# A depthwise convolution on sixteen 32x32 tiles of TensorE, four channels at once

## The chip, the cores and the metric

The kernel runs on one core of one Trainium2 chip. The metric is the device time of one launch in microseconds (us): the median of three runs of the kernel before is 9306.91 us (9300.4 to 9478.17). Views of the profile come from one more execution, recorded with the hardware profiler.

## The reference

A layer of ConvNeXt style with a mixture of experts, then an attention within each token, then a second mixture, on an image batch of 32 x 128 x 56 x 56 in float32. The change lies in the first step alone, a depthwise 7x7 convolution (each channel has its own 49 weights):

```python
x = jax.lax.conv_general_dilated(input, dw_kernel, (1, 1), ((3, 3), (3, 3)),
        feature_group_count=C, dimension_numbers=('NCHW', 'OIHW', 'NCHW')) + dw_bias[None, :, None, None]
x = jnp.transpose(x, (0, 2, 3, 1))
mu = x.mean(-1, keepdims=True)          # layer norm over the 128 channels, and so on
...
```

Everything after it (norm, choice of experts, both mixtures, attention) reads the convolution's result and is the same in both kernels.

## The kernel before

**The convolution as matrix products.** The rows of an image lie on the partitions of SBUF, 56 of them for one channel, and along a partition lie the 32 images with 62 columns each (56 and 3 of padding on both sides). Summing over the 7 rows of the filter is a product with a banded 56x56 matrix, one for each column of the filter (`band`, read backwards into `br`). The 7 columns of the filter are 7 shifted readings of the same tile, accumulated in PSUM. Even and odd output columns are computed with a trick that saves products: `products(c, 0)` takes the 4 even taps of the filter on every second column of the input ("evens"), `products(c, 1)` the 3 odd ones ("odds", 29 columns instead of 28 for each image), and `products(c, 2)` works on `xs`, the sums of neighbouring columns, with the sums of neighbouring bands ("boths", 4 taps). The even outputs are evens + odds, and the odd ones boths - evens - odds, with odds shifted by one.

**Tiles.** Two channels are worked on at once: channel `c` on partitions 0 to 55, channel `c + 64` on partitions 64 to 119. TensorE's array is cut into eight tiles of 64 rows x 32 columns. Row group `r` belongs to one channel. The four column groups `q` belong to the even and odd output rows (`i`) and to the two halves of the image batch (`b`). Each product has one PSUM tile of a bank for each channel (`cps`); the pool has eight banks.

**One turn of the loop over `c`** (64 turns): SyncE's queue starts two loads of bands (L256) and two of x (L262, `xin <- in_x_dram`, packets of one image row, 224 bytes); VectorE turns the bands round (L265, `br <- band`), GpSimd adds bands (L269) and makes `xs` (L273); TensorE works through evens, odds and boths (L244). ScalarE copies evens out of PSUM to `ea` (L281). VectorE makes the even outputs from odds in PSUM and `ea` (L285, twice per channel), replaces `ea` by boths + bias - `ea` (L289), and takes odds off again for the odd outputs (L294, twice). ScalarE's queue then starts the output's way to DRAM (L299, `conv_d <- ot`, two output rows in a packet of 448 bytes). Loads land in three rotating buffers (`nbuf`).

**Order.** Instructions on one engine run in the order that the compiler's scheduler gave them when the kernel was built, which need not be that of the text; a DMA that is started from ScalarE's queue stands in the same queue as ScalarE's copies. The next stage reads all 128 channels of a token from `conv_d` (`ct <- conv_d`, L446) and starts when the convolution has ended.

Of the kernel before, what the change touches and what calls it, by code (L numbers as in the profile page):

```python
# [8 lines left out]
F32 = mybir.dt.float32  # L9
# [3 lines left out]
ALU = mybir.AluOpType  # L13
# [4 lines left out]
P = 128  # L18
GJ = 7
GT = P * GJ  # L20
KS = 7
PAD = 3
# [3 lines left out]
def conv_attn_hybrid_kernel(  # L26
# [173 lines left out]
    HH, QP = H // 2, P // 4  # L200
    assert H <= HP and N % 2 == 0 and W % 2 == 0 and NB * (WH + 1) * 4 <= 2048
    assert H % 2 == 0 and HH <= QP
    with tc.tile_pool(name="cv_c", bufs=1) as cc, tc.tile_pool(
# [13 lines left out]
        bands = [cc.tile([P, KS, 2 * H], F32, name=f"band{i}") for i in range(nbuf)]  # L217
        turned_bands = [cc.tile([P, KS + NO, 2, QP], F32, name=f"br{i}") for i in range(nbuf)]
        xins = [cc.tile([P, N, WP], F32, name=f"xin{i}") for i in range(nbuf)]
        for i in range(nbuf):  # L220
            nc.vector.memset(bands[i], 0.0)
            nc.vector.memset(turned_bands[i], 0.0)
            nc.gpsimd.memset(xins[i], 0.0)
        cview = conv_d.rearrange("n c (h w) -> c h n w", w=2 * W)

        def products(c, part):

            bt, xi, xs = turned_bands[c % nbuf], xins[c % nbuf], sums_of_x[c]
            wide = WH + (part == 1)
            pss = [cvp.tile([P, NB, wide], F32, name="cps") for r in range(2)]  # L230
            taps = NO if part == 1 else NE
            for a in range(taps):
                for r in range(2):
                    rows = slice(r * HP, r * HP + H)
                    for b in range(2):
                        imgs = slice(b * NB, (b + 1) * NB)
                        if part < 2:
                            at_ = 2 * a + part
                            w_, m_ = at_, xi[rows, imgs, at_ : at_ + 2 * wide - 1 : 2]
                        else:  # L240
                            w_, m_ = (0, KS, KS + 1, KS + 2)[a], xs[rows, imgs, a : a + WH]
                        for i in range(2):
                            q = i * HP + b * QP
                            nc.tensor.matmul(  # L244
                                pss[r][q : q + QP], bt[rows, w_, i, :], m_,
                                start=(a == 0), stop=(a == taps - 1),
                                tile_position=(r * HP, q), skip_group_check=True,
                            )
# [3 lines left out]
        for c in range(CH):  # L252
            bt, br, xi = bands[c % nbuf], turned_bands[c % nbuf], xins[c % nbuf]
            for r in range(2):
                rows, cr = slice(r * HP, r * HP + H), r * CH + c
# [1624 lines left out]
```

## Time and profile before

| | |
|---|---|
| median of three runs | 9306.91 us |
| profiled execution: time | 9293.81 us |
| profiled execution: span, first to last instruction | 9292.1 us |
| TensorE matmul busy, whole span | 8361.1 us (90%) |
| VectorE / ScalarE / GpSimd busy, whole span | 71% / 57% / 75% |
| mean granted TensorE clock | 0.93 |
| output DMAs of the convolution (`conv_d <- ot`) issued | from 26.3 to 606.5 us |

How to read it: a row of a table of windows gives, for a stretch of time in us from the span's start, the busy time of each engine with the number of its instructions, the granted clock, the mean busy share of the 16 DMA engines (over 1 means that packets overlap) and GB/s. PE is TensorE's matmul, PEld its weight load, DVE VectorE, ACT ScalarE, POOL GpSimd, SP SyncE; a q behind the name is the engine's queue, where DMAs are issued. A float32 matmul appears as two records. A row of the groups by line gives line, engine, operation, out<-in by the program's names, shapes, count, then busy us and mean ns of one, then the idle time before and who ended it. Rows of the timeline begin with start and duration in us; neighbours of a kind are merged, with their number behind an x.

### The profile page before, as it was taken

How to read it: one execution, taken by the hardware profiler on the slowest of the kernel's cores; microseconds unless marked ns; L12 is line 12 of the kernel's file. 1: busy time of each engine (PE TensorE's matmuls, PEld its weight loads, DVE VectorE, ACT ScalarE, POOL GpSimd, SP SyncE). 2: the span in 40 equal slices, each digit the busy share in tenths (PEclk: the TensorE clock that was granted, in tenths of full speed). 3: DMA queues.
4: the chain of work that ended last, by engine and by line, in shares of the span. 5: the costliest groups of instructions: out<-in, count | busy, mean ns of one | idle time of the engine just before them, and what ended most of it. 6: DMA issues, size and time to landing. Idle time of an engine off the chain costs nothing. (4 is left out here: it accounts for less than half of the span.)

```text
span 9292.1 us, 168854 instructions
## 1 busy us (share of the span) xinstructions
PE 8361.1 (90%) x64890; PEld 6953.7 (75%) x64890; DVE 6606.0 (71%) x9020; ACT 5293.3 (57%) x13300; POOL 7015.2 (75%) x4994
## 2 busy tenths in 40 slices
PE   9996667666999999996999999999999999999879
PEld 5676455554777777775899999999999999999733
DVE  7779766665222222225999999999999999999623
ACT  1138322332333333334888888888888888888600
POOL 2235466665888888888999999999999999999500
PEclk9998788888999999998999999999999999999855
DMA  9984255555544444442000000000000000000299
GB/s 205 217 212 152 84 159 173 167 174 144 77 73 72 69 72 67 72 71 32 25 30 32 32 32 28 29 32 28 32 32 32 25 32 32 28 32 32 74 319 339
DMA packets 867126, 829.22 MB, mean 89 GB/s; under 512 B 403157, under 2 KB 758808, under 8 KB 846835
## 3 DMA queue, kind: packets, MB, share of 16 engines
q1 hardware_dynamic: 459410, 473.36, 18.2%
q0 software_dynamic: 177664, 188.81, 11.9%
q10 hardware_dynamic: 229248, 156.26, 5.7%
q8 instruction: 514, 8.42, 0.4%
q14 instruction: 290, 2.37, 0.1%
HBM read 465.46 MB, written 353.64 MB: 88 GB/s over the span
## 5 line engine op out<-in xcount | busy, mean ns | idle before, releaser
L161 POOL TENSOR_TENSOR s<-s,q 128x2048 f32<-128x2048 f32 x784 | 3600.2, 4609 | 54.1 <-DVE s L161 32.1
L161 DVE TENSOR_TENSOR s<-kv,c 128x2048 f32<-128x2048 f32 x784 | 1793.6, 2288 | 20.8 <-POOL c L161 19.2
L161 POOL DMA_INDIRECT t_d<-ys,xe x992 | 1543.2, 1556 | 331.4 <-issue 275.8
L161 DVE TENSOR_TENSOR ev<-s,kv 128x2048 f32<-128x2048 f32 x784 | 1789.8, 2283 | 1.0 <-ACT s L161 1.0
L161 ACT ACTIVATE s<-s 128x2048 f32<-128x2048 f32 x784 | 1505.9, 1921 | 463.4 <-POOL s L161 459.3
L161 PE MATMUL sm<-ident,s 128*128 128x128 f32 x12544 | 1525.2, 275 | 71.6 <-DVE oT L161 64.0
L161 PE MATMUL sm<-ident,ev 128*128 128x128 f32 x12544 | 1520.1, 275 | 1.4 <-DVE ev L161 1.4
L161 PEld LDWEIGHTS sm<-ident,s 128*128 128x128 f32 x12544 | 1398.6, 143 | 93.9 <-issue 73.7
L161 PEld LDWEIGHTS sm<-ident,ev 128*128 128x128 f32 x12544 | 1429.7, 143 | 45.9 <-DVE ev L161 3.0
L1132 ACT ACTIVATE hT<-ph,b1t 128x512 f32<-128x512 f32 (+1 forms) x992 | 679.8, 685 | 1129.6 <-PE ph L161 1122.4
L1149 DVE TENSOR_TENSOR ys<-py,b2t 128x512 f32<-128x512 f32 (+1 forms) x248 | 171.5, 692 | 1399.4 <-PE py L161 1295.5
L863 POOL DMA_INDIRECT xb_d<-xs,rd x784 | 766.0, 977 | 497.9 <-DVE xs L161 233.5
L161 PEld LDWEIGHTS py<-w,hT 128*128 128x128 f32 x7936 | 924.1, 191 | 116.9 <-issue 63.7
L161 PE MATMUL py<-w,hT 128*128 128x128 f32 x7936 | 925.3, 275 | 0.0
L161 PE MATMUL ph<-xeT,w 128*128 128x512 f32 (+1 forms) x1984 | 904.4, 599 | 0.0
L161 PEld LDWEIGHTS ph<-xeT,w 128*128 128x128 f32 x1984 | 364.1, 194 | 362.6 <-issue 359.1
L161 ACT COPY add<-px 128x512 f32<-128x512 f32 x224 | 116.0, 533 | 854.2 <-remote 474.7
L161 DVE SCALAR_TENSOR_TENSOR xs<-pa,rst,add 128x256 f32<-128x256 f32 x784 | 328.8, 479 | 344.1 <-issue 126.9
L161 PE MATMUL pa<-rw,ct 128*128 128x256 f32 x1568 | 405.1, 407 | 175.9 <-DVE xs L161 146.7
L161 PEld LDWEIGHTS pa<-rw,ct 128*128 128x128 f32 x1568 | 317.8, 207 | 295.2 <-remote 133.3
L161 PE MATMUL kv<-wq,zT 128*128 128x256 f32 x1568 | 418.6, 390 | 53.1 <-DVE ev L161 53.1
L244 PE MATMUL cps<-xin,br 56*32 56x448 f32 (+1 forms) x7168 | 440.9, 585 | 18.2 <-POOL xs L273 13.4
(348 smaller groups left out, 13723.4 us busy)
## 6 DMA issues: line engine op xcount, KB each, us to landing
ct<-conv_d SPq DMA_DIRECT2D x192, 448.0 KB
xin<-in_x_dram SPq DMA_DIRECT2D x128, 392.0 KB
conv_d<-ot ACTq DMA_DIRECT2D x256, 196.0 KB
t_d<-xs ACTq DMA_DIRECT2D x112, 448.0 KB
tr<-t_d SPq DMA_DIRECT2D x112, 448.0 KB
to<-t_d SPq DMA_DIRECT2D x32, 1568.0 KB
out_dram<-oo ACTq DMA_DIRECT2D x32, 1568.0 KB
xg<-in_x_dram SPq DMA_DIRECT2D x96, 448.0 KB
```

What stands on the lines that cost most here:

```text
L161: r = getattr(self.engine, name)(*a, **k)
L244: nc.tensor.matmul(pss[r][q : q + QP], bt[rows, w_, i, :], m_, start=(a == 0), stop=(a == taps - 1), tile_position=(r * HP, q), skip_group ...
L863: s = nc.gpsimd.indirect_dma_start(out=xb_d, out_offset=bass.IndirectOffsetOnAxis(ap=idx, axis=0), in_=row, in_offset=None, bounds_check=R ...
L1132: nc.scalar.activation(hT[:, f, :, :rows], ph[:, :, :rows], AF.Gelu, bias=b1t[:, f : f + 1])
L1149: nc.vector.tensor_tensor(ys[:rows], py[:rows], across(b2t, SB)[:rows], ALU.add)
```

## The change

Four channels are worked on at once (`R4`), in 32 turns instead of 64. A partition now holds two neighbouring rows of an image (`pi`), so a channel needs 28 of 32 partitions, and the array is cut into sixteen tiles of 32 rows x 32 columns. Each tap needs two matmuls, one for each of the two rows on a partition. A product has four PSUM tiles, one for each channel, in the same pool of eight banks.

The two rows lie next to each other in DRAM, so x is loaded in packets of 448 bytes into a tile `raw` without padding (three buffers); ScalarE copies `raw` into the padded `xin` (two buffers). Bands are loaded with every second row and the row after it for each partition. `xs` has two buffers instead of three. VectorE turns and GpSimd adds bands for each of the two rows apart.

ScalarE now copies odds to SBUF as well (`od`), and both copies stand in the text right behind their product; VectorE's two operations on odds read `od` instead of PSUM. The sums, their order for one output, and the way out to DRAM are as before.

```diff
--- before.py
+++ after.py
@@ -197,7 +197,7 @@
     WH, CH = W // 2, C // 2
     NE, NO = (KS + 1) // 2, KS // 2
     BL = (KS - 1) * 2 * H + H
-    HH, QP = H // 2, P // 4
+    HH, QP, R4 = H // 2, P // 4, 4
     assert H <= HP and N % 2 == 0 and W % 2 == 0 and NB * (WH + 1) * 4 <= 2048
     assert H % 2 == 0 and HH <= QP
     with tc.tile_pool(name="cv_c", bufs=1) as cc, tc.tile_pool(
@@ -214,76 +214,96 @@
         nc.sync.dma_start(bias, dw_bias.partition_broadcast(P))
 
         nbuf = 3
-        bands = [cc.tile([P, KS, 2 * H], F32, name=f"band{i}") for i in range(nbuf)]
-        turned_bands = [cc.tile([P, KS + NO, 2, QP], F32, name=f"br{i}") for i in range(nbuf)]
-        xins = [cc.tile([P, N, WP], F32, name=f"xin{i}") for i in range(nbuf)]
+        bands = [cc.tile([P, 2, KS * 2 * H], F32, name=f"band{i}") for i in range(nbuf)]
+        turned_bands = [cc.tile([P, 2, KS + NO, 2, QP], F32, name=f"br{i}") for i in range(nbuf)]
+        raws = [cc.tile([P, N, 2, W], F32, name=f"raw{i}") for i in range(nbuf)]
+        xins = [cc.tile([P, N, 2, WP], F32, name=f"xin{i}") for i in range(2)]
         for i in range(nbuf):
             nc.vector.memset(bands[i], 0.0)
             nc.vector.memset(turned_bands[i], 0.0)
-            nc.gpsimd.memset(xins[i], 0.0)
+            nc.gpsimd.memset(raws[i], 0.0)
+        for xi in xins:
+            nc.gpsimd.memset(xi, 0.0)
         cview = conv_d.rearrange("n c (h w) -> c h n w", w=2 * W)
 
         def products(c, part):
 
-            bt, xi, xs = turned_bands[c % nbuf], xins[c % nbuf], sums_of_x[c]
+            bt, xi, xs = turned_bands[c % nbuf], xins[c % 2], sums_of_x[c]
             wide = WH + (part == 1)
-            pss = [cvp.tile([P, NB, wide], F32, name="cps") for r in range(2)]
+            pss = [cvp.tile([P, NB, wide], F32, name="cps") for r in range(R4)]
             taps = NO if part == 1 else NE
             for a in range(taps):
-                for r in range(2):
-                    rows = slice(r * HP, r * HP + H)
-                    for b in range(2):
-                        imgs = slice(b * NB, (b + 1) * NB)
-                        if part < 2:
-                            at_ = 2 * a + part
-                            w_, m_ = at_, xi[rows, imgs, at_ : at_ + 2 * wide - 1 : 2]
-                        else:
-                            w_, m_ = (0, KS, KS + 1, KS + 2)[a], xs[rows, imgs, a : a + WH]
-                        for i in range(2):
-                            q = i * HP + b * QP
-                            nc.tensor.matmul(
-                                pss[r][q : q + QP], bt[rows, w_, i, :], m_,
-                                start=(a == 0), stop=(a == taps - 1),
-                                tile_position=(r * HP, q), skip_group_check=True,
-                            )
+                for pi in range(2):
+                    for r in range(R4):
+                        rows = slice(r * QP, r * QP + HH)
+                        for b in range(2):
+                            imgs = slice(b * NB, (b + 1) * NB)
+                            if part < 2:
+                                at_ = 2 * a + part
+                                w_, m_ = at_, xi[rows, imgs, pi, at_ : at_ + 2 * wide - 1 : 2]
+                            else:
+                                w_, m_ = (0, KS, KS + 1, KS + 2)[a], xs[rows, imgs, pi, a : a + WH]
+                            for i in range(2):
+                                q = i * HP + b * QP
+                                nc.tensor.matmul(
+                                    pss[r][q : q + QP], bt[rows, pi, w_, i, :], m_,
+                                    start=(a == 0 and pi == 0), stop=(a == taps - 1 and pi == 1),
+                                    tile_position=(r * QP, q), skip_group_check=True,
+                                )
             return pss
 
         sums_of_x = {}
-        for c in range(CH):
-            bt, br, xi = bands[c % nbuf], turned_bands[c % nbuf], xins[c % nbuf]
-            for r in range(2):
-                rows, cr = slice(r * HP, r * HP + H), r * CH + c
+        for c in range(C // R4):
+            bt, br, raw, xi = bands[c % nbuf], turned_bands[c % nbuf], raws[c % nbuf], xins[c % 2]
+            for r in range(R4):
+                rows, cr = slice(r * QP, r * QP + HH), r * (C // R4) + c
                 nc.sync.dma_start(
-                    bt[rows].rearrange("p a b -> p (a b)")[:, :BL],
+                    bt[rows, :, :BL],
                     bass.AP(
-                        band_d.tensor, band_d.offset + cr * KS * 2 * H, [[1, H], [1, BL]]
+                        band_d.tensor, band_d.offset + cr * KS * 2 * H,
+                        [[2, HH], [1, 2], [1, BL]],
                     ),
                 )
                 nc.sync.dma_start(
-                    xi[rows, :, PAD : PAD + W], x[:, cr].rearrange("n h w -> h n w")
-                )
-            nc.vector.tensor_copy(
-                br[:, :KS, :, :HH],
-                bt[:, :, :H][:, :, ::-1].rearrange("p k (h i) -> p k i h", i=2),
-            )
-            nc.gpsimd.tensor_tensor(
-                br[:, KS:, :, :HH], br[:, 2:KS:2, :, :HH], br[:, 1 : KS - 1 : 2, :, :HH], ALU.add
-            )
-            xs = sums_of_x[c] = cv.tile([P, N, WP // 2], F32, name="xs")
-            nc.gpsimd.tensor_tensor(xs, xi[:, :, 0::2], xi[:, :, 1::2], ALU.add)
+                    raw[rows].rearrange("p n i w -> p n (i w)"),
+                    x[:, cr].rearrange("n (h i) w -> h n (i w)", i=2),
+                )
+            for pi in range(2):
+                nc.vector.tensor_copy(
+                    br[:, pi, :KS, :, :HH],
+                    bt[:, pi].rearrange("p (a b) -> p a b", a=KS)[:, :, :H][:, :, ::-1].rearrange(
+                        "p k (h i) -> p k i h", i=2
+                    ),
+                )
+                nc.gpsimd.tensor_tensor(
+                    br[:, pi, KS:, :, :HH], br[:, pi, 2:KS:2, :, :HH],
+                    br[:, pi, 1 : KS - 1 : 2, :, :HH], ALU.add,
+                )
+            nc.scalar.copy(xi[:, :, :, PAD : PAD + W], raw)
+            xs = sums_of_x[c] = cv.tile([P, N, 2, WP // 2], F32, name="xs", bufs=2)
+            nc.gpsimd.tensor_tensor(xs, xi[:, :, :, 0::2], xi[:, :, :, 1::2], ALU.add)
             evens = products(c, 0)
+            eas = []
+            for r in range(R4):
+                ea = cv.tile([P, NB, WH], F32, name="ea", bufs=2 * R4)
+                nc.scalar.copy(ea, evens[r])
+                eas.append(ea)
             odds = products(c, 1)
+            ods = []
+            for r in range(R4):
+                od = cv.tile([P, NB, WH + 1], F32, name="od", bufs=2 * R4)
+                nc.scalar.copy(od, odds[r])
+                ods.append(od)
             boths = products(c, 2)
-            ot = cv.tile([P, NB, 2, W], F32, name="ot", bufs=3)
-            for r in range(2):
-                cr = r * CH + c
-                ea = cv.tile([P, NB, WH], F32, name="ea", bufs=4)
-                nc.scalar.copy(ea, evens[r])
-                mine = slice(r * HP, (r + 1) * HP)
+            for r in range(R4):
+                cr, ea, od = r * (C // R4) + c, eas[r], ods[r]
+                if r % 2 == 0:
+                    ot = cv.tile([P, NB, 2, W], F32, name="ot", bufs=3)
+                mine = slice(r % 2 * HP, (r % 2 + 1) * HP)
                 for i in range(2):
                     of = slice(i * HP, (i + 1) * HP)
                     nc.vector.scalar_tensor_tensor(
-                        ot[mine, :, i, 0::2], odds[r][of, :, :WH], bias[of, cr : cr + 1], ea[of],
+                        ot[mine, :, i, 0::2], od[of, :, :WH], bias[of, cr : cr + 1], ea[of],
                         ALU.add, ALU.add,
                     )
                 nc.vector.scalar_tensor_tensor(
@@ -292,10 +312,10 @@
                 for i in range(2):
                     of = slice(i * HP, (i + 1) * HP)
                     nc.vector.tensor_tensor(
-                        ot[mine, :, i, 1::2], ea[of], odds[r][of, :, 1:], ALU.subtract
+                        ot[mine, :, i, 1::2], ea[of], od[of, :, 1:], ALU.subtract
                     )
                 for b in range(2):
-                    q = r * HP + b * QP
+                    q = r % 2 * HP + b * QP
                     nc.scalar.dma_start(
                         cview[cr][:, b * NB : (b + 1) * NB, :],
                         ot[q : q + HH].rearrange("p n i w -> p n (i w)"),
```

## The prediction

> **What bounds the kernel now.** I first asked the table of windows where the convolution lies and which engine fills it, because the change touches only that stage.
>
> ```profile
> core 0: us, PE busy (x) PEld busy (x) DVE busy (x) ACT busy (x) POOL busy (x), PEclk, DMA share, GB/s
> ...
> 100.00:200.00 100.00, 100.00 (x1960) 57.98 (x1952) 81.10 (x125) 9.98 (x21) 26.05 (x22) 1.00 1.04 216
> ```
>
> The stage runs from 13.4 us (first matmul in the timeline) to about 607 us (last output issued at 606.5 us): 6.4% of the span. In it TensorE is never idle, at full granted clock; VectorE is at 81%, ScalarE at 10%. The DMA engines are full as well, so two resources could be the limit. A limit of 2% (about what a measurement of this kernel can tell from no change) is 186 us, almost a third of the stage.
>
> A busy TensorE may still be starved, since matmuls overlap. So I looked in the timeline at the bursts of weight loads, one for each round of eight tiles:
>
> ```profile
> 22.20 0.14 PEld L244 LDWEIGHTS cps<-xs,br 56*32 56x32 f32 x8 [0.24 <-issue]
> 22.57 0.14 PEld L244 LDWEIGHTS cps<-xs,br 56*32 56x32 f32 x8 [0.24 <-issue]
> ...
> 25.33 0.17 PEld L244 LDWEIGHTS cps<-xin,br 56*32 56x32 f32 x8 [0.25 <-issue]
> 25.74 0.19 PEld L244 LDWEIGHTS cps<-xin,br 56*32 56x32 f32 x8 [0.25 <-issue]
> ...
> 27.84 0.19 PEld L244 LDWEIGHTS cps<-xin,br 56*32 56x32 f32 x8 [0.24 <-issue]
> 28.27 0.19 PEld L244 LDWEIGHTS cps<-xin,br 56*32 56x32 f32 x8 [0.24 <-issue]
> ```
>
> The reader sees rounds of 0.374 us (packed `xs`, 448 columns), 0.416 us (`xin` with step 2, 448 columns) and 0.430 us (the same, 464 columns). The time goes with the columns, so TensorE is bound by streaming, not by waits or issue. A pair of channels takes 8 x 0.416 + 6 x 0.430 + 8 x 0.374 = 8.90 us; the timeline repeats every 8.97 us (`xin` groups at 303.37, 312.38 and 321.30). TensorE sets the pace and DMA only just keeps up.
>
> Next, what must keep out of its way, from the groups of instructions by line (busy time, mean ns of one, idle time before):
>
> ```profile
> L285 DVE SCALAR_TENSOR_TENSOR ot<-cps,bias,ea 64x448 f32<-64x448 f32 x215 | 147.2, 684 | 81.8 <-ACT ea L281 75.7 <-DMA conv_d<-ot 1.4
> L294 DVE TENSOR_TENSOR ot<-ea,cps 64x448 f32<-64x448 f32 x216 | 135.5, 627 | 5.1
> ...
> L289 DVE SCALAR_TENSOR_TENSOR ea<-cps,bias,ea 128x448 f32<-128x448 f32 x108 | 73.9, 684 | 3.5
> L281 ACT COPY ea<-cps 128x448 f32<-128x448 f32 x105 | 52.3, 537 | 418.2 <-DMA conv_d<-ot 209.4 <-DMA xin<-in_x_dram 174.3 <-PE cps L244 33.7
> ```
>
> and, from the waits of 100 to 600 us and ScalarE's timeline, how long a copy stands behind output DMAs in its queue, and what TensorE lost by it:
>
> ```profile
> ACT ea L281 <- DMA conv_d<-ot: 230.3, 16, 15.9
> ...
> PE cps L244 <- ACT ea L281: 0.6, 2, 0.4
> ```
> ```profile
> 570.83 10.61 ACTq L299 DMA_DIRECT2D conv_d<-ot  x8
> ```
>
> The copies come up to 15.9 us late, and TensorE does not notice (0.6 us in 500): eight banks hold four products, so a bank has three more products' time to be emptied.
>
> **The change, part by part.** TensorE: per four channels 11 taps x 2 row parities x 4 row groups x 2 x 2 = 352 matmuls in place of 176, each in two records, over 16 tiles in place of 8. That is 704 / 16 = 44 rounds, as now (352 / 8 = 44). With the measured rounds: 16 x 0.416 + 12 x 0.430 + 16 x 0.374 = 17.80 us per four channels, against 2 x 8.97 = 17.94 now. So TensorE gains nothing, if 16 tiles stream at once. The trace shows two row groups at once, never four; the bounds are the same round (0) and two half rounds one after the other (+17.8 us per group). I take the first: four column tiles and two row groups overlap completely here.
>
> Issue: a round must take 32 instructions instead of 16, 12.5 ns each. The nearest row is in the last stage:
>
> ```profile
> 8860.29 0.81 PEld L1822 LDWEIGHTS p_fo<-fw,fhT 128*32 128x32 f32 x32 [1.71 <-ACT fhT L1818]
> 8860.29 1.08 PE L1822 MATMUL p_fo<-fw,fhT 128*32 128x128 f32 x32 [1.51 <-ACT fhT L1818]
> ```
>
> Here 64 instructions start within some 0.85 us: 13 ns each, and that pace is its own 128-column streaming. So the cost lies between nothing and a round of 32 x 13.2 = 0.422 us (+0.02 us mean on 1408 rounds, +30 us). I take nothing, since inside a round starts lie closer still.
>
> A rule of the Trainium skill speaks against it: "TensorE: Matmul & The Clock Gate", under "Wait — 56ns, not 53.3ns?", says that starts never come closer than about 25 ns. Taken for matmuls alone it gives rounds of 16 x 25 = 0.40 us, some +13 us in all; taken for weight loads too, 0.80 us and +560 us. The p_fo row above, at 13 ns for each of both kinds, does not bear out the second. Part 3 of that page reports 10.6 times for a pack of 16 tiles; no run here shows it.
>
> Banks: each product now takes four of the eight, so two products are in flight and each must be emptied within the next one's time. Evens: four copies on ScalarE, 4 x 0.54 = 2.1 us, while odds take 12 x 0.43 = 5.2. Odds: the new copies, 2.2 us, while boths take 16 x 0.374 = 6.0. Boths: VectorE, while the next evens take 6.7. Its chain there is 4 of L289 and, between them, 6 of L294: 4 x 0.72 + 6 x 0.66 = 6.8 us with the gaps of the timeline. Before that it must have finished 8 of L285; these wait for the odds' copies (0.65 us after odds end) and take 8 x 0.72 = 5.8, of which boths hide 5.4. L285 and L294 now read SBUF. The nearest SBUF-only row, the 128x224 scalar_tensor_tensor `rest<-w,lgs` at 384 ns, stands 151 ns above its streaming, where L285 stands 218 ns above its own (0.96 elements per ns, from L294's 627 ns at 448 and the 2288 ns of a 2048-wide tensor_tensor), so I bound L285 at 618 to 685 ns. The loop odds, copy, L285s, boths' chain is 5.2 + 0.8 + 5.2 to 5.8 + 6.8 = 18.0 to 18.6 us against TensorE's 17.8. I take a stall of 0.6, so 18.4 us per group, +0.46 on 32 groups: +15 us.
>
> ScalarE: the spread copy of 128x3584 costs 3.25 us (537 ns at 448 and 1921 ns at 2048 elements in `s<-s` give 0.865 ns each). With eight sums' copies (4.3) that is 7.6 us per group, plus eight output issues of 0.31 us (their median) to 1.33 us (10.61 / 8). 10.1 to 18.2 of 17.8 us: it fits unless the issues stay blocked. The spread copy is hidden by prefetch over three `raw` buffers; shown late, it delays evens by its 3.25 us.
>
> DMA:
>
> ```profile
> q1 hardware_dynamic: 199169, 59.32, 62.5%
> q10 hardware_dynamic: 104326, 45.34, 39.2%
> ```
>
> Over 500 us x 16 engines a 448-byte output packet costs 39.2% x 8000 / 104326 = 30 ns, an SP packet 25 ns on the mean, nearly all of them 224-byte reads of x. Half as many x packets at 25 to 50 ns relieve the engines by 0 to 90 of 290 engine-us per group; at 30 ns, some 70, about a quarter. It hides under TensorE already, so this earns nothing directly; it makes the issues on ScalarE's queue less blocked. Bands keep their bytes and number.
>
> GpSimd: `xs` twice as wide, half as often, 3.7 us per group under 17.8. VectorE's two band copies of 0.56 us are as many as now and fit the 4 us before the next odds' copies.
>
> Ends: five memsets of 3584 or 3968 elements take 3 x 3.16 + 2 x 3.50 = 16.5 us in place of 5.2 (1748 ns for 1984). The first `xin` is clean at some 14.5 us, then comes its 3.25 us copy: first matmul at about 18 instead of 13.4, +4.5. After the last boths VectorE has four rows of 2.0 us to finish, not two: +4.
>
> **Sum**: 4.5 + 15 + 4 = +23.5 on the profiled execution's 9293.8 us = 9317. The median of the runs, 9306.9, lies 13 us above that execution, so 9330.
>
> **Rivals.** (1) The array or its issue doesn't carry 16 tiles: slower. Over 2% from rounds of 0.395 + 186 / 1408 = 0.53 us, 61 instructions per us; the most that lasts over several microseconds in the trace is about 43 (16 in 0.374), and only the short p_fo burst shows 75. At 43, rounds of 0.74 us: +490 us, about 9800. Two half rounds: +570. For: never shown here. Against: no sign of an issue limit. (2) Bank turns stall TensorE, because sums' copies stand behind blocked output issues on ScalarE. Four issues of 1.33 = 5.3 us per group: +170 us, 9490; with a spread copy in front too, 8.6 us: +275, 9600. It decides from 5.8 us of stall per group. For: waits of 15.9 us now, and half the banks' slack. Against: relieved DMA, and copies that are ready early. (3) Faster: if reading x at step 2 reached the packed pace under less DMA, 28 x 0.042 x 32 = 38 us come off, about 9290. Even a stage of pure 0.374 rounds saves under 70 us, so 2% faster has no mechanism.
>
> **How the numbers follow.** Forecast (stage within some 100 us of today's, mild stalls) 0.68; rival 3 0.07, of it 0.01 past 2%; rival 2 0.13, of it 0.08 past 2%; rival 1 0.12, all past it. Hence faster 0.01, within 2% 0.79, slower 0.20. The range runs from rival 3, 9280, to 9500, where only the heavier stalls are left out; the forecast's own is 9300 to 9400.
>
> **What would show it.** Right: weight-load bursts of 16 every 0.37 to 0.43 us, groups every 17.8 to 19 us, DMA share below 0.9, first matmul near 18 us, the stage's end near 630 us. Wrong: longer rounds with TensorE never idle (rival 1), or idle TensorE on `ea`, `od` or boths' readers (rival 2).

## The result and the profile after

| | before | after |
|---|---|---|
| median of the runs | 9306.91 us | 9635.17 us (9622.97 to 9640.35, 4 runs) |
| profiled execution: span | 9292.1 us | 9621.2 us |
| mean granted TensorE clock, whole span | 0.930 | 0.924 |
| first matmul of the convolution starts | 13.4 us | 25.8 us |
| last matmul of the convolution starts | 601.5 us | 918.6 us |

The change makes the kernel slower by 3.5%: ratio 1.035, 95% interval 1.0337 to 1.0363. The forecast was 9330 us with a range up to 9500. The run of 9478.17 us of the kernel before was in a slower state of the chip, and the ratio leaves it out. Of the 329 us by which the span grew, 305 lie between the convolution's first and last matmul (588.1 us before, 892.8 after), 12 ahead of its first and 12 behind its last.

The table of windows of the kernel after, with the same columns as before:

```profile
core 0: us, PE busy (x) PEld busy (x) DVE busy (x) ACT busy (x) POOL busy (x), PEclk, DMA share, GB/s
...
300.00:400.00 100.00, 85.15 (x2474) 53.23 (x2478) 60.03 (x77) 22.47 (x31) 17.68 (x11) 0.95 0.70 146
500.00:600.00 100.00, 88.09 (x2497) 57.71 (x2498) 58.47 (x76) 23.25 (x33) 14.81 (x10) 0.90 0.70 145
```

TensorE was busy for 100 of 100 us before. Now it stands still for 12 to 15, the granted clock dips to 0.90, and every other engine and the DMA engines have room: no unit that does work is full. The waits of TensorE between 100 and 800 us (engine, operation, what was waited for: us, times, longest) show almost nothing that it waited for:

```profile
PE cps L248 <- issue: 103.5, 56, 4.9
PE cps L248 <- DVE ea L309: 1.7, 3, 0.8
```

"issue" means that the matmul waited for nothing that the profile records. In TensorE's timeline such stops look like this, with the first burst of the stage ahead of them:

```profile
25.82 8.99 PE L248 MATMUL cps<-xin,br 28*32 28x448 f32 x223 [25.82 <-ACT xin L282]
...
411.43 3.35 PE L248 MATMUL cps<-xin,br 28*32 28x448 f32 x87
417.15 4.42 PE L248 MATMUL cps<-xin,br 28*32 28x448 f32 x128 [2.36 <-issue]
423.09 1.45 PE L248 MATMUL cps<-xin,br 28*32 28x464 f32 x34 [1.52 <-issue]
```

Between two stops lie exactly 128 matmul records. With a weight load each, that is 256 instructions. The DMA queues of 100 to 800 us (packets, MB, share of 16 engines) hold one more user:

```profile
q1 hardware_dynamic: 102475, 59.48, 45.9%
q10 hardware_dynamic: 88705, 38.55, 23.6%
q8 instruction: 135, 2.21, 1.4%
```

Queue 8 brings instructions, in packets of 16,384 bytes. In the stage 176 of them come for 45,056 matmuls and weight loads: 256 instructions a packet. In the kernel before it is 88 for 22,528, and its list of queues for 100 to 600 us shows one packet per 6.5 us:

```profile
q8 instruction: 77, 1.26, 1.1%
```

Laid beside the matmul starts of the kernel after, from the trace's records (us):

```
matmul starts stop    next packet of queue 8    starts go on
414.23                414.22, took 1.43         417.15
420.99                420.63, took 1.20         423.09
438.62                436.93, took 1.46         439.93
```

In all, 88 spacings between matmul starts are over 0.6 us, and they sum to 172.6 us (before: 9 and 10.7). Nearly all lie at one place modulo 128 in the order of the matmuls (it creeps from 95 to 78 over the stage). Of those over 1 us, matmuls go on 1.29 to 1.69 us after the end of the last instruction packet (10th to 90th percentile). So the theory to be tried was: **A, the supply of instructions**. A block of 256 lasts 6.5 us with eight tiles and some 3.7 us with sixteen, and blocks do not come that fast while data crowds the DMA engines.

The remaining 892.8 - 172.6 = 720.2 us are longer too, by 142.8 over before's 577.4. Rounds of sixteen tiles take a median of 0.450 us on `xs` and 0.466 on `xin`, where rounds of eight took 0.378 and 0.420: **B, the rounds themselves**. (A round is counted here from one matmul start to the sixteenth, or eighth, after it; medians are of rounds at the full granted clock without a spacing over 0.6 us. Rounds of sixteen scatter: a tenth of those on `xs` takes under 0.40 us and a tenth over 0.57.) And the groups and timelines showed two more suspects:

```profile
L314 DVE TENSOR_TENSOR ot<-ea,od 64x448 f32<-64x448 f32 x242 | 240.4, 993 | 5.6
L305 DVE SCALAR_TENSOR_TENSOR ot<-od,bias,ea 64x448 f32<-64x448 f32 x248 | 178.5, 720 | 278.7 <-ACT od L295 275.0
L309 DVE SCALAR_TENSOR_TENSOR ea<-cps,bias,ea 128x448 f32<-128x448 f32 x123 | 81.3, 682 | 50.3 <-PE cps L248 48.3
L289 ACT COPY ea<-cps 128x448 f32<-128x448 f32 x124 | 57.1, 546 | 549.6 <-DMA conv_d<-ot 301.9 <-DMA band<-band_d 144.2 <-PE cps L248 103.5
```

The copies of evens, L289, still come late behind outputs (**C, ScalarE's copies behind its output issues**). And the subtraction L314 has grown from 627 to 993 ns. VectorE's timeline and GpSimd's side by side show why:

```profile
410.30 4.78 DVE L314 TENSOR_TENSOR ot<-ea,od 64x448 f32<-64x448 f32 x2
```
```profile
410.22 3.49 POOL L284 TENSOR_TENSOR xs<-xin 128x1984 f32<-128x1984 f32 x1 [0.47 <-PE cps L248]
```

Where L314 meets the making of `xs`, one takes 2.68 us on the mean (42 of 256), elsewhere 0.638. Since the change both of its operands lie in SBUF; before, with one in PSUM, it took 0.632 us beside `xs` and 0.625 without (**D, VectorE held by GpSimd**).

### The profile page after: what moved, and what is told of

Read it like the earlier page. It is cut to its first block, busy times and chain, and to the rows that moved or that the text cites. A ratio compares the mean times of both kernels' runs of the same rounds, so it can differ in the third digit from the quotient of the medians.

```text
span 9621.2 us, 191164 instructions
## 1 busy us (share of the span) xinstructions
PE 8559.6 (89%) x76154; PEld 7093.4 (74%) x76154; DVE 6696.3 (70%) x9020; ACT 5455.5 (57%) x13460; POOL 7039.5 (73%) x4964
## 5 line engine op out<-in xcount | busy, mean ns | idle before, releaser
L248 PE MATMUL cps<-xin,br 28*32 28x448 f32 (+1 forms) x14336 | 546.5, 625 | 117.4 <-issue 87.8
L248 PEld LDWEIGHTS cps<-xin,br 28*32 28x32 f32 x14336 | 332.6, 107 | 303.3 <-issue 198.0
```

What stands on the lines that cost most here:

```text
L248: nc.tensor.matmul(pss[r][q : q + QP], bt[rows, pi, w_, i, :], m_, start=(a == 0 and pi == 0), stop=(a == taps - 1 and pi == 1), tile_posi ...
```

## The experiments

Kernel by kernel, counted from the trace's records of the matmuls. "Against before" is the run's time less that of the kernel before, run beside it on the same chip (9302 us beside e1 to e4, 9074 beside e5 to e8, 9069 beside e9 to e12, 9284 beside e13 to e15; only times taken together are compared). Each kernel was profiled in one execution; only e11, e12 and e15 and the kernels before and after were run more often. Where an expectation names a theory by a letter, it is one of the four above. The last column is what passes between the end of the last instruction packet and the matmul after a spacing over 1 us, 10th to 90th percentile.

| kernel | against before, us | first to last matmul, us | spacings over 0.6 us: number, sum | rest, us | after a packet's end, us |
|---|---|---|---|---|---|
| before | | 588.1 | 9, 10.7 | 577.4 | |
| after | +328 | 892.8 | 88, 172.6 | 720.2 | 1.29 to 1.69 |
| e4_split | +278 | 861.3 | 133, 246.9 | 614.4 | 1.31 to 1.64 |
| e1_wide | +184 | 754.5 | 180, 195.7 | 558.9 | 1.39 to 10.05 |
| e2_noload | +166 | 739.2 | 37, 43.8 | 695.4 | 0.74 to 3.81 |
| e3_rinner | +328 | 893.3 | 87, 164.9 | 728.5 | 1.35 to 1.65 |
| e7_tiles8 | +182 | 756.5 | 72, 122.3 | 634.2 | 1.31 to 5.79 |
| e8_tiles12 | +208 | 781.4 | 80, 143.9 | 637.6 | 1.37 to 5.11 |
| e6_od | +126 | 706.9 | 61, 115.3 | 591.6 | 1.39 to 8.32 |
| e5_noxs | +145 | 715.8 | 70, 100.9 | 614.9 | 1.03 to 5.54 |
| e13_pool | +46 | 606.4 | 42, 46.4 | 560.0 | 1.11 to 8.48 |
| e14_fetch | +329 | 892.8 | 83, 167.6 | 725.2 | 1.34 to 1.69 |

Two things help to read it. In every row the whole's difference is the stage's plus that of the first matmul's start to within 15 us, so stages may be compared across chips to that much. And a spacing over 0.6 us need not be a stop: in stretches in which the granted clock was halved (0.50 in the profile), the ordinary pause between two rounds gets that long. That makes 96.4 of the 195.7 us of e1_wide, 20 us or less in the other rows, and nothing in e4_split. Such stretches add up to 113 us of the stage in the kernel after, 130 in e1_wide, 10 in e2_noload and 3 in e13_pool.

**Twice the instructions in the kernel before.** Each matmul of the old kernel is cut in two of half the columns: 8 tiles, old copies, old loads, but 512 instructions where 256 were. (The sums come out wrong by it.)

```diff
             for a in range(taps):
+                for h in range(2):
...
+                            lo = h * NB // 2
+                            imgs = slice(b * NB + lo, b * NB + lo + NB // 2)
...
-                                pss[r][q : q + QP], bt[rows, w_, i, :], m_,
+                                pss[r][q : q + QP, lo : lo + NB // 2], bt[rows, w_, i, :], m_,
```

> The kernel before, eight tiles of 64 x 32, with each matmul cut into two of half the columns (eight images each): twice the instructions, the same columns in all, the same two row groups, banks, copies and DMAs. Theory A: the stage becomes as long as in the changed kernel or longer, since x comes in 224-byte packets and the DMA engines are fuller: gaps at every 128th matmul record or so, stage 850 to 950 us, the whole 9560 to 9660. Theories B and C: nothing but a little issue cost, 9300 to 9340.

Measured: 9580.42 us, +278. TensorE's waits between 100 and 800 us:

```profile
PE cps L246 <- issue: 161.8, 112, 3.4
```

The old kernel with nothing changed but the number of instructions gets the new kernel's stops: 246.9 us in spacings, at one place modulo 128 (it creeps evenly from 95 to 1 over the stage), and matmuls that go on 1.31 to 1.64 us after an instruction packet. The pace of issue as such is not the limit: between stops the rounds of 16 instructions take 0.190 us on `xs` (median), 11.9 ns each, less than the 14.1 ns of a sixteen-tile round (0.450 / 32).

**Half the instructions in the kernel after.** One matmul serves both output row parities, in tiles of 32 rows x 64 columns; everything else stays. (Output rows land in another order.)

```diff
-                            for i in range(2):
-                                q = i * HP + b * QP
-                                nc.tensor.matmul(
-                                    pss[r][q : q + QP], bt[rows, pi, w_, i, :], m_,
+                            q = b * HP
+                            nc.tensor.matmul(
+                                pss[r][q : q + HP],
+                                bt[rows, pi, w_].rearrange("p i q -> p (i q)"), m_,
```

> The changed kernel with tiles of 32 rows x 64 columns: one matmul makes the even and the odd output rows together, so there are 176 matmuls per four channels instead of 352, with the same 44 rounds of the same columns, the same four row groups and the same banks, copies and DMAs. (Output rows land on other partitions than the later steps assume, so the convolution's rows are mixed up.) Theory A, instruction supply: TensorE uses up its blocks of 256 instructions (128 matmul records) faster than they are fetched. Then the gaps of 1 to 5 us between matmul starts (172.6 us in all in the changed kernel) vanish, rounds fall to 0.37 to 0.43 us, a group takes 18 to 19 us, and the whole 9310 to 9370. Theory B, the array: four row groups at once stretch the rounds themselves. Then rounds stay near 0.5 us, a group at 22, the whole near 9450. Theory C, bank turns: the waits for copies on ScalarE and for VectorE's reading of boths stay, the whole near 9600.

Measured: 9486.30 us, +184, more than A alone allowed (9370). Rounds take 0.393 and 0.421 us, with all four row groups in use. Of the stops at block boundaries hardly one is left. 34 spacings over 1 us remain, 92.4 us in all, and 30 of them (86.5 us) stand at one place of a turn, 12 matmul records into odds, where the text asks for the fourth channel's bank. They have a name, the first of TensorE's two waits between 100 and 700 us:

```profile
PE cps L247 <- DVE ea L309: 60.2, 26, 5.4
PE cps L247 <- issue: 1.7, 3, 0.7
```

So with half the instructions the supply is off the path, and banks that VectorE frees late (D) take its place. This is rival 2's kind of stall, which the stops of A had covered.

**The kernel after without data loads.** x and bands are loaded in the first three turns only and used again.

```diff
+                if c < nbuf:
-                nc.sync.dma_start(
+                    nc.sync.dma_start(
                         bt[rows, :, :BL],
...
```

> The changed kernel with bands and x loaded only in the first three turns; later turns work on the old data in the three buffers (so most channels get others' results). SyncE's queue is silent from about 40 us on; instructions of all engines, copies and output DMAs stay. Theory A, in the form that blocks of instructions come late because they queue behind data on the DMA engines: the gaps of 1 to 5 us shrink to a few, some 150 us less, about 9470, with rounds as long as in the changed kernel. If the blocks are slow by themselves, gaps stay: about 9600. Theory C: the copies depend on output DMAs in ScalarE's queue, which stay; gaps stay, 9550 to 9620.

Measured: 9468.35 us, +166. All 45,056 instructions are still fetched; the window of 300 to 500 us:

```profile
300.00:500.00 200.00, 195.14 (x6227) 144.78 (x6224) 152.39 (x192) 61.66 (x81) 46.18 (x27) 1.00 0.33 72
```

TensorE is busy for 97.6% at full clock. Blocks are 3.95 us apart (median, and 5.8 at the 95th percentile; after: 4.52 and 7.8), and of 172.6 us in spacings 43.8 remain, no longer tied to a packet: 35.1 of them stand at the fourth bank of odds, as in e1_wide. "issue" is gone from TensorE's waits (100 to 700 us):

```profile
PE cps L248 <- DVE ea L310: 15.3, 26, 0.9
```

So it is the data that is loaded beside them that makes blocks late. Rounds are as long as in the kernel after (0.452 and 0.471), so B is another thing: at full clock, (695.4 - 577.4) = 118 us over the old kernel.

**Another order of the tiles.** The four row groups innermost, so that successive matmuls go to different rows of the array.

```diff
                 for pi in range(2):
-                    for r in range(R4):
-                        rows = slice(r * QP, r * QP + HH)
-                        for b in range(2):
...
+                    for b in range(2):
+                        imgs = slice(b * NB, (b + 1) * NB)
+                        for i in range(2):
+                            for r in range(R4):
```

> The changed kernel with the loop over the four row groups innermost: matmuls in a row go to different row groups, instead of four in a row to the same. All counts are the same. If weight loads in a row to one row group are what stretches the rounds (pauses of about 100 ns, the length of one weight load), rounds fall from 0.5 to 0.40 us; by theory A the blocks are then used up faster and the gaps grow, so the whole falls less, to 9500 to 9600. If the rounds are stretched by something else (theory B, or issue), nothing changes: 9620 within 30 us.

Measured: 9629.86 us, +328, rounds of 0.441 and 0.471. The order decides nothing.

**Eight and twelve of the sixteen tiles.** The tiles of odd output rows (e7_tiles8), or of odd rows and the second half of the images (e8_tiles12), get only the first tap, and of that only one of the two rows on a partition; the rest of their sums is left out. The edit is that of e7_tiles8; in e8_tiles12 the first line reads `few = i == 1 and b == 1`.

```diff
+                                few = i == 1
+                                if few and (a or pi):
+                                    continue
...
+                                    start=(a == 0 and pi == 0), stop=few or (a == taps - 1 and pi == 1),
```

> The changed kernel, where the matmuls of the odd output rows (half of the sixteen tiles) run for the first tap alone (the odd output rows are wrong). 38 of 44 rounds have eight tiles of 32x32, four row groups and two column groups, 16 instructions a round. Open is why rounds of sixteen tiles take 0.49 us even with the fetch unhindered, where eight tiles take 0.41. If it is the number of tiles or instructions in a round, most rounds take 0.40 to 0.42 us. If it is the 32x32 form of tiles, 0.49 stays. Fetch gaps vanish in both cases; waits as in e1_wide stay: the whole 9430 to 9500.

> As e7_tiles8, but only a quarter of the tiles (odd rows of the second half of the images) stop after the first tap: 38 of 44 rounds have twelve tiles and 24 instructions. If each instruction costs some 15 ns (0.49 / 32), rounds are bound by columns, 0.41 us. If a window of instructions ahead is too short for weight loads from some number of tiles on, rounds lie between 0.41 and 0.49. Blocks of 256 instructions last 4.3 us, so a part of the fetch gaps comes back: the whole 9450 to 9560.

Measured: 9255.39 (+182) and 9281.85 us (+208). Rounds on `xs` and `xin` have medians of 0.393 and 0.420 us with eight tiles, 0.395 and 0.422 with twelve, 0.450 and 0.466 with sixteen. All three use all four row groups. So four row groups do stream at once, and the lengthening comes between twelve and sixteen. What makes it stays open: not the fetch (e2_noload), not four row groups (twelve tiles), not the order (e3_rinner), not the pace of instructions (e4_split). With twelve tiles, 24 instructions a round, the stops at block boundaries are there again: TensorE's waits on "issue" between 100 and 700 us, with eight tiles and then with twelve, are

```profile
PE cps L251 <- issue: 6.2, 6, 1.9
```
```profile
PE cps L251 <- issue: 53.6, 29, 4.7
```

The granted clock narrows B further. These are stretches at half clock without a stop, of e1_wide (eight tiles) and of the kernel after (sixteen):

```profile
267.10:273.90 6.80, 6.17 (x64) 2.23 (x72) 1.82 (x3) 1.84 (x4) 0.00 (x0) 0.50 0.98 232
```
```profile
265.34:272.16 6.82, 6.61 (x128) 3.40 (x128) 4.63 (x6) 0.00 (x0) 3.56 (x2) 0.50 0.93 162
```

Sixteen tiles start twice the matmuls there: a round takes a median of 0.747 us (112 rounds of the kernel after), with eight tiles 0.773 (127 rounds of e1_wide on `xin`). So sixteen tiles do stream at once, and what lengthens their rounds at full clock is something else, which hides at half clock and which no run here names.

**The copy of odds in the kernel before.** Only `od` is added to the old kernel.

```diff
             odds = products(c, 1)
+            ods = []
+            for r in range(2):
+                od = cv.tile([P, NB, WH + 1], F32, name="od", bufs=4)
+                nc.scalar.copy(od, odds[r])
+                ods.append(od)
...
-                        ot[mine, :, i, 0::2], odds[r][of, :, :WH], bias[of, cr : cr + 1], ea[of],
+                        ot[mine, :, i, 0::2], ods[r][of, :, :WH], bias[of, cr : cr + 1], ea[of],
```

> The kernel before, with one part of the change alone: odds are copied to SBUF by ScalarE (od), and VectorE's two operations on odds read that copy. Theory D: some of the 256 subtractions overlap GpSimd's xs (1.84 us here) and take up to 2.5 us; their mean rises from 627 to 750 to 1000 ns. With four products in the banks TensorE does not notice much: 9290 to 9330. If od's copies come too late behind output DMAs (theory C), TensorE gets gaps and the whole takes 9350 or more.

Measured: 9199.70 us, +126, as theory C had it: this piece of the change costs 1.4% by itself. TensorE's waits between 100 and 580 us:

```profile
PE cps L244 <- ACT od L279: 58.9, 15, 5.1
```

Banks of odds were freed by VectorE before; now they wait for ScalarE, whose copies stand behind output DMAs in its queue (C). D shows as well: both of VectorE's operations on odds read two operands from SBUF, and take 1.34 and 1.40 us beside `xs`, 0.64 and 0.68 elsewhere.

**Off with what hid behind A.** e5_noxs is e1_wide with `xs` made in the first two turns only (D gone). e13_pool has in addition the outputs issued from GpSimd's queue and the sums of bands made on VectorE (C gone). `xs` is out of date in both.

```diff
+            if c < 2:
+                xs = sums_of_x[c] = cc.tile([P, N, 2, WP // 2], F32, name=f"xs{c}")
...
+            else:
+                xs = sums_of_x[c] = sums_of_x[c % 2]
```
```diff
-                nc.gpsimd.tensor_tensor(
+                nc.vector.tensor_tensor(
                     br[:, pi, KS:, :, :HH], br[:, pi, 2:KS:2, :, :HH],
...
-                    nc.scalar.dma_start(
+                    nc.gpsimd.dma_start(
                         cview[cr][:, b * NB : (b + 1) * NB, :],
```

> e1_wide with GpSimd's sums xs made only in the first two turns and used again later (so boths are wrong for the other channels); everything else is e1_wide. There the fetch gaps are gone, but a group still takes 24.3 us, and TensorE waits at the odds for VectorE's reading of boths. Theory D: VectorE's subtraction L314 has both operands in SBUF since the change, and the first two after boths stand still while GpSimd makes xs (3.3 us on the mean where they overlap, 0.65 where they don't); with GpSimd silent they take 0.65 us, boths are read in 6.8 us, and a group falls to 18 to 19 us, the whole to 9310 to 9340. Theory C, the copies behind output DMAs in ScalarE's queue: the 24 us stay, about 9480.

> e5_noxs (tiles of 32x64, xs made only in the first two turns) with the output DMAs started from GpSimd's queue and the small band sums moved from GpSimd to VectorE, so that ScalarE's queue holds copies alone, SyncE's loads alone. Theory C: TensorE's waits for ea vanish, matmuls of the stage take 575 to 620 us instead of 716, the whole 0 to 50 us above the kernel before on the same chip. Without theory C: 700 us or more, 130 us above it.

Measured: 9218.90 (+145, between the two forecasts) and 9330.05 us (+46, as C had it); the stage shrinks from 754.5 to 715.8 to 606.4 us. In e5_noxs L314's successor takes 0.64 us throughout, and ScalarE's waits between 100 and 580 us show what is left:

```profile
ACT ea L292 <- DMA conv_d<-ot: 296.1, 19, 17.1
```

In e13_pool (300 to 500 us) TensorE is full again:

```profile
300.00:500.00 200.00, 193.74 (x3776) 89.30 (x3768) 154.26 (x257) 72.47 (x99) 59.61 (x88) 1.00 0.95 212
```

Four channels at once, 28 rows on a row group and two image rows in a packet are thus carried at nearly the old pace, with half the matmuls of the kernel after, `xs` made in two turns only and copies that stand behind no output.

**And sixteen tiles with C and D gone.** The kernel after, with `xs`, outputs and sums of bands as in e13_pool.

> The changed kernel with sixteen tiles and all its matmuls, changed otherwise as e13_pool (outputs from GpSimd's queue, band sums on VectorE, xs only in the first two turns). If the fetch of instructions sets the pace by itself, matmuls of the stage take 820 to 900 us and gaps between matmul starts stand at one place of each 128 records, the whole 230 to 330 us above the kernel before. If fetch and late copies had to come together, 650 to 760 us and 80 to 180 us above.

Measured: 9613.00 us, +329; the stage takes 892.8 us, as in the kernel after. Between 100 and 700 us:

```profile
PE cps L248 <- issue: 88.1, 39, 3.9
```

With C and D taken away nothing is won: in the kernel after they cost next to nothing, because A with B comes last. Against e13_pool only the tiles' shape differs, 32x32 for 32x64: 286 us.

**Two that missed.** e9_sp (e5_noxs) and e10_fetch (the kernel after without `xs`) were to take C away by issuing outputs from SyncE's queue.

```diff
-                    nc.scalar.dma_start(
+                    nc.sync.dma_start(
                         cview[cr][:, b * NB : (b + 1) * NB, :],
```

> e5_noxs (tiles of 32x64, xs made only in the first two turns) with the output DMAs started from SyncE's queue instead of ScalarE's. Theory C, ScalarE's copies of evens and odds stand behind output DMAs: TensorE's waits for ea vanish, matmuls of the stage take 575 to 610 us instead of 716, the whole lies within 30 us of the kernel before on the same chip. Without theory C: still some 145 us above it.

> The changed kernel with its sixteen tiles and all its matmuls, without theory C's and D's causes: output DMAs from SyncE's queue, and xs made only in the first two turns (boths are wrong for the other channels). Theory A, the fetch of instructions alone sets the pace: matmuls of the stage still take 830 to 890 us (893 in the changed kernel), the whole 250 to 330 us above the kernel before. If copies and VectorE caused a good part of the loss, the stage falls to some 740 us or less, as in the run without loads.

Measured: 9387.98 (+319) and 9574.64 us (+506), stages of 895.1 and 1079.3 us. SyncE's queue in e9_sp between 100 and 600 us:

```profile
SPq L322 <- DVE ot L317: 215.2, 48, 14.0
```

Outputs wait there for VectorE, and the loads of the turns to come stand behind them. TensorE then waited for `xin` (157.3 us). Neither run says anything on A or C.

**Three tries at a version.** e11_best: tiles of 32x64, even and odd columns of `xin` each packed by ScalarE, three operations of VectorE per channel, `xs` on VectorE, outputs on SyncE's queue. e12_packed: the old kernel with packed columns and outputs on SyncE's queue. e15_best: e11_best with outputs on GpSimd's queue, sums of bands on VectorE, and a sum of `ea` and `od` made ahead, so that boths go straight to `ot`:

```diff
+                nc.vector.tensor_tensor(ea, ea, od[:, :, 1:], ALU.add)
                 nc.vector.scalar_tensor_tensor(
-                    ea, boths[r], bias[:, cr : cr + 1], ea, ALU.add, ALU.subtract
+                    ot[:, :, 1::2], boths[r], bias[:, cr : cr + 1], ea, ALU.add, ALU.subtract
                 )
-                nc.vector.tensor_tensor(ot[:, :, 1::2], ea, od[:, :, 1:], ALU.subtract)
...
-                        nc.sync.dma_start(
+                        nc.gpsimd.dma_start(
```

> A version of the changed kernel with the causes taken away: tiles of 32x64, output DMAs from SyncE's queue with one row in a packet (224 bytes), three VectorE operations on 128 partitions per channel instead of five, xs on VectorE, and even and odd columns of x laid apart by ScalarE's copy, so that TensorE reads packed columns only. Theories A, C and D: 44 rounds of 0.375 to 0.395 us, 16.6 to 17.2 us per group, matmuls of the stage 535 to 560 us, the whole 0 to 40 us below the kernel before. If the DMA engines bind (as many and as small output packets as x packets before, some 298 of 16 x 17.9 engine-us per group), the stage takes 590 to 610 us and the whole 0 to 40 us above.

> The kernel before with x loaded into raw tiles, even and odd columns laid apart by ScalarE's copy, and output DMAs from SyncE's queue; tiles of 64x32 and packets as before. TensorE reads packed columns only: 22 rounds of 0.375 to 0.39 us, 8.35 us per pair instead of 8.97, the stage 35 to 40 us shorter, the whole 20 to 40 us below the kernel before. If the DMA engines bind, whose busy share is 1.05 already, the pair stays at 8.9 to 9.0 us and the whole within 15 us.

> e11_best with the outputs from GpSimd's queue, band sums on VectorE, and one VectorE operation instead of two between the end of boths and a free bank (odds are added to ea before). By theories A, C and D nothing is left in TensorE's way but the DMA engines: 44 rounds of 0.375 to 0.395 us, matmuls of the stage 535 to 600 us, the whole from 50 us below the kernel before to 20 above. If the output DMAs from GpSimd's queue are slow to issue (16 per group, some 1 us each in the indirect DMAs of later stages), they become the pace: 620 to 700 us, 40 to 120 us above.

Measured: e11_best 9357.61 us, 1.032 of before (1.0303 to 1.0337); e12_packed 9434.39, 1.0403 (1.0385 to 1.042); e15_best 9379.34, 1.0104 (1.0087 to 1.0121). The first two wait for `xin` behind outputs, like e9_sp. In e15_best VectorE waits for output buffers, and GpSimd's queue for the transfers (100 to 600 us, then GpSimd's timeline):

```profile
DVE ot L304 <- DMA conv_d<-ot: 196.8, 74, 6.4
```
```profile
321.21 5.39 POOL L314 DMA_DIRECT2D conv_d<-ot  x8 [2.58 <-DMA conv_d<-ot]
```

With tiles of 32x64 an output row parity is a group of partitions of its own, so packets are one row of 224 bytes and outputs are sixteen DMAs per turn instead of eight, 0.67 us of GpSimd's time each. No version beat the kernel before.

## Why the prediction was wrong, step by step

- **Issue: "I take nothing". This step failed.** Its bounds, nothing to 30 us, came from 64 instructions of p_fo in some 0.85 us. Such a burst shows how fast instructions are started that are already there, and e4_split bears that out (11.9 ns each). It does not show how fast they arrive. The stage was to take 1408 instructions in 17.8 us, 79 per us; the old one took 39 (704 in 17.94 us). What arrived is a mean of 256 per 5.1 us (892.8 / 176). The row that tells it, q8 above with one packet per 6.5 us, stood in the same list that I quoted for q1 and q10. Spacings cost 162 us more than before. The Trainium skill, "Runtime: NRT & Kernel Launch", section "Instruction fetch mechanics", calls the cost of crossing a 16 KiB boundary "mostly hidden". The kernel before bears that out (10.7 us of spacings in 588.1), the kernel after does not (172.6 in 892.8).
- **The rounds, 0.374 to 0.430 us.** Held up to twelve tiles. At sixteen the medians are 0.450 and 0.466, above the upper bound of 0.422 that I gave; at full clock that is 118 us on 1408 rounds (e2_noload), where the bound allowed 30. The 25 us left of the 143 fit the granted clock, 0.94 on the mean of the stage against 0.99 in the kernel before and in e2_noload, but no run took that apart.
- **Rival 1** had the right sign, and its point of decision, 0.53 us per round, was passed: 892.8 / 1408 = 0.63. Of its causes neither was right: no two half rounds (a round takes 0.45 to 0.47 us at full clock), and no limit of 43 instructions per us in issuing (e4_split takes 84). With 0.12 for it, the range was let end at 9500, below its 9800.
- **Bank turns, +15 us.** In the kernel after they cost TensorE 1.7 us in 700, because a starved TensorE gives everyone time. Once A is gone they are large: 754.5 - 606.4 = 148 us of stage in e1_wide, for C and D together, with what the halved clock adds there. So rival 2's mechanism was there, covered. Its price for ScalarE's part, 170 to 275 us, stands against 715.8 - 606.4 = 109 us.
- **VectorE on SBUF.** I bounded L305 at 618 to 685 ns; away from `xs` it takes 683. And I missed that both operations became open to being held by GpSimd. The Trainium skill says so: "GPSIMD Engine Reference", section 1, Specifications, names contention with VectorE's instructions that have two SBUF inputs. The 2.68 against 0.638 us above agree with it.
- **DMA relieved "by about a quarter". Wrong, at the bound.** A 448-byte packet of x takes 43.4 ns on the mean where a 224-byte one took 22.1, so the x of four channels costs the engines 3584 x 43.4 ns = 156 engine-us, against 7168 x 22.1 = 158 before. The share fell to 0.70 only because the turn got longer; in e13_pool it is 0.95 again, at 212 GB/s.
- **Ends.** First matmul at 25.8 us, not 18. The copy took 3.24 us, as expected, but `raw` landed only at 21.2, and a load of ScalarE's tables (1.28 us) stood before the copy. I had counted the memsets, the last of which for the first `xin` would have let it start at 18.2; what came last were the first turn's four loads of x, of which SyncE's queue issued the last two at 12.2 and 13.7 us, behind three and four loads of bands. At the other end I had put +4 us; it was +12: the first load of `ct` in the next stage starts 20.2 us after the convolution's last matmul, where it was 8.1. VectorE had finished at 926.5, but the last turn's eight outputs hold ScalarE's queue for 14.8 us where the last four held it for 3.2 (before, then after):

```profile
604.14 3.16 ACTq L299 DMA_DIRECT2D conv_d<-ot  x4
```
```profile
920.60 14.77 ACTq L319 DMA_DIRECT2D conv_d<-ot  x8
```
- **ScalarE's spread copy**, 3.25 us: measured 3.284. Hidden, as predicted.

## What to carry to other kernels

Cutting a product into smaller tiles keeps the arithmetic and doubles the instructions, so divide the stage's time by its instruction blocks and look at how often the profile's instruction queue gets one, beside how full the DMA engines are: here 6.5 us per block was fine and 3.7 was not. A wait on "issue" that came back after the same number of instructions was a fetch here, not an engine's limit. And what costs nothing behind a starved engine (a copy behind output DMAs, a second SBUF operand beside GpSimd) is priced only once that engine is fed.

## What the runs showed of the hardware that I had not expected

- Instruction blocks compete with data: with loads running, blocks come 3.5 to 7.8 us apart (5th to 95th percentile, after); without, 3.5 to 5.8, with a median of 3.95. After a stop, matmuls go on about 1.45 us after a block's packet has ended.
- Sixteen tiles in flight lengthen a round from about 0.395 to 0.450 us (packed `xs`) at full granted clock, twelve do not; at half clock sixteen do not either (0.747 us, with eight 0.773 on `xin`).
- VectorE's operations with both operands in SBUF stand still while GpSimd adds two SBUF tiles (2.68 against 0.638 us), those with one operand in PSUM do not (0.632 against 0.625).
- Packets of 448 bytes into SBUF took twice the time of packets of 224 (43.4 and 22.1 ns), so merging two rows in one packet freed nothing.
- Which queue issues the outputs moved the stage by up to 289 us: 895.1 us from SyncE's (e9_sp), 715.8 from ScalarE's (e5_noxs), 606.4 from GpSimd's (e13_pool, with the sums of bands moved to VectorE).
